# Query tokens and slot rows turned by VectorE and carried through DRAM, with a new order around the first batch's gathering

## The chip, the cores and the metric

The kernel runs on one core of one Trainium2 chip. The metric is device time in microseconds, the median of several executions; the same program runs with the same inputs each time. The profile is of one execution of its own.

## The reference

Two layers over x of shape (2, 1024, 256), all in float32. The batch is cut into four quads of 512 tokens (quads 0 and 1 are batch 0). What matters here is layer 1 and its soft mixture of experts:

```
x = x + xattn0(layernorm(x), ctx)          # layer 0, windowed attention, 8 heads
x = x + ffn0(layernorm(x))                 # layer 0, 8 groups of two linear maps
h = layernorm(x);  q = h @ Wq.T            # layer 1: 16 heads of 16
scores = sigmoid(q @ k.T * scale);  x = x + (scores @ v) @ Wo.T
xn = rms_norm(layernorm(x), gamma_x);  se = rms_norm(slot_embeds, gamma_slot)   # 1024 slots
logits   = xn @ se.T                                    # (b, s, 1024)
dispatch = softmax(logits, over tokens);  slots = dispatch.T @ xn
y        = gelu(slots @ w1) @ w2
combine  = softmax(logits, over slots);   x = x + combine @ y
```

## The kernel before

A tile holds 128 rows; a quad has QT = 4 of them, D = 256 is DC = 2 chunks of 128, and the 1024 slots are EC = 8 chunks. PSUM is used as two groups ("sides") of four banks each; a tile that needs a bank waits until an earlier user of it has been read.

Most instructions are placed on their engines by a scheduler that follows the program's order and what is ready by its own estimate. Inside `tc.manual_schedule(engines=...)` the engines named take the order of the program as it is written, and `tc.keep_in_program_order` does it for one instruction. Each engine then works its queue in order; an instruction that waits holds up those behind it. All the DMAs named here are issued by SyncE (SP), also in order.

The work in order of time (lines are those of the kernel before):

- Layer 0. `weigh` and `attend` do the attention of a quad. The two linear maps of a group are multiplied together once (`product`, L774, `pmt`), their bias follows in `bias_rows` (L805, VectorE) and `bias` (L811 to L813, `pbs` and `bs`), and `feed_forward` (L826 to L839, `po`) applies the product to `hT_f`. `layernorm` normalises a quad on VectorE (`hn`) and calls `transposed` (L126, `pt`), which turns it by eight TensorE transposes into two PSUM banks; two copies (L127) then bring it to `hT`. Who copies, ScalarE or VectorE, is left to the scheduler.
- Layer 1's attention. `layernorm(xq[q], "a1_q", 1)` makes `hT_a` for the queries of each quad, `queries` (L1150, `pq`) projects them, then for each half c of the heads: scores (L1217, `psg`, four matmuls on 32 rows each), tanh on ScalarE (`sg`, L1226), `poT` (L1251), `oT` (L1258), and `output` (L1164, `pf`) adds to x.
- Slots. `turn_slot_rows(h)` scales half of the slot embeddings (L1094) and calls `turned` (L135 and L144): VectorE transposes 32x32 squares of a tile in place, four instructions for 512 rows, and 16 DMAs of 32 KB bring the squares to the rows where they belong, as `seT`. In the attention's loop this happens once before it and once in quad 0. `turn_tokens` does the same for the tokens of each quad (`tr_m`, `xhT`).
- Logits (L224, `pl`): 128 matmul records of 512 columns with `seT` as the moving operand. VectorE reduces each bank twice (L232, L243) into row maxima and into `rmax`, the largest per slot.
- Maxima of batch 0. `largest(0)` turns `rmax` on TensorE (L296, `pm`), reduces it (L297) and multiplies it into eight diagonal 128x128 squares (L301, `dg`); `spread(0)` sums these over the rows by two matmuls with ones (L315, `pb`), which gives each row all 1024 maxima (`mb`). Then `less` (L349) adds them to the negated logits, tile by tile on GpSimd, and `dispatch` (L352) takes the exponential on ScalarE.
- Maxima of batch 1 go another way: `largest_by_moves` and `spread_by_moves` use VectorE, a DRAM row (`mrow`) and a DMA that reads the row into all partitions. For this batch `less` is on VectorE for tiles 3 and 6.
- Gathering. `gather(b, c)` (L360, `psl`) sums over the eight token tiles of a batch for slot chunk c; VectorE divides (`rz`, `sl`), `turn_slots` turns the result on TensorE (L379, `pst`) and writes `slT` with the scale (L387). During the gathering of batch 0, `turn` (L276, L285) turns the combine weights of chunks on VectorE, with 16 DMAs for each call.
- `hidden` (L435, `pmh`), `processed` and `combined` (L505, `pp` and `pc`) are fast matrix products with seven products for eight, whose sums of operands are made by `sum_slots` (L422 to L426) and others on VectorE.

Of the kernel before, what the change touches and what calls it, by code (L numbers as in the profile page):

```python
# [9 lines left out]
FP = mybir.dt.float32  # L10
AF = mybir.ActivationFunctionType
ALU = mybir.AluOpType
# [33 lines left out]
SQ = 32  # L46
R4 = P // SQ


@with_exitstack  # L50
def tile_kernel(
# [54 lines left out]

    seT = const.tile([P, 2, DC, 512], FP, tag="seT", name="seT")

# [11 lines left out]

    def transposed(src, dst, name, side=0):

        for c in range(DC):
            pt = bank(f"pt_{name}_{c}", side)
            for t in range(QT):
                nc.tensor.transpose(pt[:, ts(t, P)], src[:, t, ts(c, P)], ident)  # L126
            nc.any.tensor_copy(dst[:, c, :], pt)  # L127

    def turned(src, dst, tr, late=False):

        for t in range(QT):
            turn = nc.vector.transpose(  # L135
                tr[:, :, :, t, :].rearrange("p r c n -> p c r n"),
                src[:, t, 0:D].rearrange("p (c r n) -> p c r n", c=DC, r=R4),
            )
            if late:
                tc.keep_in_program_order(turn)  # L140
        to = dst.rearrange("p c (t i n) -> p (c t) i n", t=QT, i=R4)
        for i in range(R4):
            for r in range(R4):
                nc.sync.dma_start(  # L144
                    out=to[ts(r, SQ), :, i, :],
                    in_=tr[ts(i, SQ), r].rearrange("p c t n -> p (c t) n"),
                )


# [62 lines left out]
    def logits(b, s):  # L212
# [8 lines left out]
        for n in range(NSLOT // 512):  # L221
            pl = bank(f"pl_{b}_{s}_{n}", 0)
            for dc in range(DC):
                nc.tensor.matmul(  # L224
                    pl,
                    lhsT=xhTs[q][:, dc, ts(t, P)],
                    rhs=seT[:, n, dc, :],
                    start=(dc == 0),
                    stop=(dc == DC - 1),
                )  # L230
# [59 lines left out]
    def largest(b):  # L290

        mT = stat.tile([P, EC], FP, tag="mT", name=f"mT_{b}")
        for h in range(EC // 4):
# [5 lines left out]
            )  # L299
        dg = pools["mw"].tile([P, EC, P], FP, tag="dg", name=f"dg_{b}")  # L300
        nc.vector.tensor_tensor(  # L301
            dg,
            ident.unsqueeze(1).to_broadcast([P, EC, P]),
            mT.unsqueeze(2).to_broadcast([P, EC, P]),
            ALU.mult,
# [3 lines left out]
    def spread(b):  # L309

        dgf = mTs[b].rearrange("p c n -> p (c n)")
        mb = pools["md"].tile([P, NSLOT], FP, tag="mb", name=f"mb_{b}")
        for n in range(NSLOT // 512):
            pb = bank(f"pb_{b}_{n}", 1)
            nc.tensor.matmul(pb, lhsT=ones, rhs=dgf[:, ts(n, 512)], start=True, stop=True)  # L315
            copy(n, mb[:, ts(n, 512)], pb)
        mbs[b] = mb
# [15 lines left out]
    def spread_by_moves(b):  # L333

        w, m4 = moved[b]
        m2, m3 = w[0:SQ, 1, 5 * SQ : 6 * SQ], w[0:SQ, 1, 6 * SQ : 7 * SQ]
        tc.keep_in_program_order(
            nc.vector.tensor_reduce(m2, m4.rearrange("n i c -> n c i"), AX.X, ALU.max)
        )
        nc.vector.transpose(m3, m2)  # L340
# [6 lines left out]
    def less(b, s):  # L347
        engine = nc.vector if b == 1 and s in (3, 6) else nc.gpsimd
        engine.tensor_tensor(lgs[b][s], lgs[b][s], mbs[b], ALU.add)  # L349
# [5 lines left out]

    def gather(b, c):

        pz = bank(f"psl_{b}_{c}", 0)
        for s in range(ST):
            nc.tensor.matmul(  # L360
                pz[:, 0:XW],
                lhsT=lgs[b][s][:, ts(c, P)],
                rhs=xhs[b * QB + s // QT][:, s % QT, :],
                start=(s == 0),
                stop=(s == ST - 1),
            )
        rz = stat.tile([P, 1], FP, tag="rz", name=f"rz_{b}_{c}")
        nc.vector.reciprocal(rz, pz[:, D : D + 1])  # L368
# [60 lines left out]
    def hidden(b):  # L429
# [18 lines left out]

        p1s = [alone(0, 0)]
        turn_slots(b, EC - 1)  # L450
        p1s.append(alone(0, 1))
        p2 = alone(1, 0)
        sum_slots(b)
        hs = {}
# [263 lines left out]
    with (  # L718
# [14 lines left out]

        def layernorm(xt, name, side=0):
            mv, rstd = moments(xt, name)
            hn = lnp.tile([P, QT, D], FP, tag="hn", name=f"hn_{name}")
            for t in range(QT):
                nc.vector.tensor_scalar(  # L738
                    hn[:, t, :], xt[:, t, :], mv[:, t, 0:1], rstd[:, t : t + 1],
                    ALU.subtract, ALU.mult,  # L740
                )
            hT = lnp.tile([P, DC, QN], FP, tag="hT", name=f"hT_{name}")
            transposed(hn, hT, name, side)
            return hT
# [74 lines left out]
        def norm_ff(q, side=0):  # L819
            hTfs[q] = layernorm(xq[q], f"f0_{q}", side)  # L820

# [246 lines left out]
        with (  # L1068
# [21 lines left out]
            def turn_slot_rows(h):  # L1090
# [7 lines left out]
                tr = lnp.tile([P, R4, DC, QT, SQ], FP, tag="tr", name=f"tr_se_{h}")  # L1098
                turned(se[:, ts(h, QT), :], seT[:, h], tr, late=True)

# [42 lines left out]
            hTs, qTs, oTs = {}, {}, {}  # L1143

            def queries(q):
                qTs[q] = a1.tile([P, C1, QN], FP, tag="qT", name=f"qT_{q}")
                for c in range(C1):
                    pq = bank(f"pq_{q}_{c}", 1)
                    for dc in range(DC):
                        nc.tensor.matmul(  # L1150
                            pq,
                            lhsT=wq1s[:, dc, ts(c, P)],
                            rhs=hTs[q][:, dc, :],
                            start=(dc == 0),
# [20 lines left out]

            slot_norms()
            hTs[0] = layernorm(xq[0], "a1_0", 1)
            product(7)
            norm_ff(NQ - 1)
            turn_slot_rows(0)  # L1180
            bias_rows(7)

# [19 lines left out]
            queries(0)  # L1202
            bias(7)
            work = ExitStack()
            for q in range(NQ):
                b = q * QN // S
                oTs[q] = a1.tile([P, C1, QN], FP, tag="oT", name=f"oT_{q}")
                for c in range(C1):
                    if c == 1 and q == 0:
                        turn_slot_rows(1)  # L1210
                    if c == 0 and q > 1:
# [17 lines left out]
                    if c == 0:  # L1229
                        if q == 0:  # L1230
# [6 lines left out]
                            )  # L1237
                        if q + 1 < NQ:
                            hTs[q + 1] = layernorm(xq[q + 1], f"a1_{q + 1}", 1)
                        if q > 0:  # L1240
# [25 lines left out]

    ctx.enter_context(tc.manual_schedule(engines={mybir.EngineType.Activation}))
    open_keep(1)
    open_pool("slp", side="right")
    for u in range(1, B * ST + 2):  # L1270
        b, s = divmod(u, ST)
# [18 lines left out]

    largest_by_moves(1)
    work.close()
# [7 lines left out]
    for b in range(B):  # L1300
        slTs[b] = pools["slp"].tile([P, DC, NSLOT], FP, tag="slT", name=f"slT_{b}")
        for c in range(EC):
            gather(b, c)
            if c > 0:
                turn_slots(b, c - 1)
            if b == 0 and c in (1, 3, 5):
                turn(c // 4, c // 2 % 2, c == 5)
            if b == 1 and c % 2 == 0:
                turn(QB + c // 4, c // 2 % 2, True)
            if b == 0 and c == 0:  # L1310
                spread_by_moves(1)
                sum_weights()
            if b == 0:
                less(1, c)
                if c > 0:
                    dispatch(1, c - 1)
        if b == 0:
            dispatch(1, ST - 1)
        hidden(b)
        with tc.manual_schedule(engines={mybir.EngineType.DVE, mybir.EngineType.PE}):  # L1320
            processed(b)
            combined(b)
# [70 lines left out]
```

## Time and profile before

The median is 440.9 us (three runs, 440.69 to 441.31).

| quantity | value |
|---|---|
| profiled execution | 441.36 us |
| its span on the core | 439.6 us |
| granted TensorE clock | 1.00 |
| TensorE busy | 428.7 us (98%) |
| VectorE busy | 332.0 us (76%) |
| ScalarE busy | 113.7 us (26%) |
| GpSimd busy | 81.9 us (19%) |
| DMA packets | 101025, of them 94850 under 512 B |

In the profile PE is TensorE's matmuls, PEld its weight loads, DVE VectorE, ACT ScalarE, POOL GpSimd, and SPq the DMAs that SyncE issues. A matmul in float32 shows as two records. A matmul's record lasts longer than its share of the engine, because matmuls are pipelined; the chain of waits gives the distance from one group to the next, and that is the share. A row of the chain has the start, the length, the engine and the line. A row of a timeline has the start, the length, the instruction, and in brackets how long the engine was idle before it and what ended that. A row of the waits has the total, the number of times and the longest. A row of DMA issues has the size of one and the median time from issue to landing.

### The profile page before, as it was taken

How to read it: one execution, taken by the hardware profiler on the slowest of the kernel's cores; microseconds unless marked ns; L12 is line 12 of the kernel's file. 1: busy time of each engine (PE TensorE's matmuls, PEld its weight loads, DVE VectorE, ACT ScalarE, POOL GpSimd, SP SyncE). 2: the span in 40 equal slices, each digit the busy share in tenths (PEclk: the TensorE clock that was granted, in tenths of full speed). 3: DMA queues.
4: the chain of work that ended last, by engine and by line, in shares of the span. 5: the costliest groups of instructions: out<-in, count | busy, mean ns of one | idle time of the engine just before them, and what ended most of it. 6: DMA issues, size and time to landing. Idle time of an engine off the chain costs nothing.

```text
span 439.6 us, 6389 instructions
## 1 busy us (share of the span) xinstructions
PE 428.7 (98%) x2356; PEld 318.5 (72%) x2356; DVE 332.0 (76%) x737; ACT 113.7 (26%) x212; POOL 81.9 (19%) x82
## 2 busy tenths in 40 slices
PE   6999999999999999999999989999999999999997
PEld 5778888888755545444458854699999884499997
DVE  0477989899475766998887679995995478796856
ACT  1212143203254451333561165510000003530000
POOL 3011332224122022200695760000000000000000
PEclk9999999999999999999999999999999999999999
DMA  8996495500303032221025843333003666600002
GB/s 268 415 421 281 171 373 245 192 1 1 48 2 48 13 46 39 39 31 28 0 73 167 127 67 47 52 52 47 0 1 100 98 92 96 95 1 0 2 1 95
DMA packets 101025, 42.61 MB, mean 97 GB/s; under 512 B 94850, under 2 KB 97026, under 8 KB 99586
## 3 DMA queue, kind: packets, MB, share of 16 engines
q1 hardware_dynamic: 100994, 42.22, 36.2%
q8 instruction: 18, 0.29, 0.3%
q14 instruction: 13, 0.10, 0.1%
HBM read 28.55 MB, written 2.10 MB: 70 GB/s over the span
## 4 chain that ended last, share of the span: by engine, by line
PE 81%; DVE 14%; POOL 1%; ACT 1%; DMA 1%; issue 1%; ACTq 0%; POOLq 0%
PE psl L360 13%; PE pl L224 12%; PE pp L505 11%; PE pc L505 11%; PE pmh L435 11%; PE pmt L774 5%; DVE b2z L805 5%; PE pq L1150 3%; PE pf L1164 3%; PE psg L1217 2%; PE poT L1251 2%; PE po L832 2%; DVE hn_f L738 1%; DVE bn_f L114 1%; DVE bn_a L114 1%; PE pt_a L126 1%
## 5 line engine op out<-in xcount | busy, mean ns | idle before, releaser
L774 PE MATMUL pmt<-wg 128*128 128x256 f32 x256 | 60.3, 394 | 3.8 <-DMA wg<-in_wff_dram 3.8
L360 PE MATMUL psl<-xh,lg 128*128 128x258 f32 x256 | 58.2, 381 | 0.0
L774 PEld LDWEIGHTS pmt<-wg 128*128 128x128 f32 x256 | 50.0, 198 | 11.2 <-DMA wg<-in_wff_dram 4.3
L224 PE MATMUL pl<-seT,xhT 128*128 128x512 f32 x128 | 55.9, 593 | 0.0
L360 PEld LDWEIGHTS psl<-xh,lg 128*128 128x128 f32 x256 | 47.4, 190 | 7.2 <-issue 0.5
L224 PEld LDWEIGHTS pl<-seT,xhT 128*128 128x128 f32 x128 | 24.2, 190 | 29.1 <-issue 24.9
L349 POOL TENSOR_TENSOR lg<-lg,mb 128x1024 f32<-128x1024 f32 x14 | 34.5, 2501 | 30.4 <-DVE mb L173 26.7
L505 PEld LDWEIGHTS pp<-ms,mh 128*128 128x128 f32 x256 | 29.4, 192 | 1.0 <-issue 1.0
L505 PE MATMUL pp<-ms,mh 128*128 128x128 f32 x256 | 29.7, 276 | 0.0
L247 ACT ACTIVATE ec<-lg,nm 128x1024 f32<-128x1024 f32 x16 | 18.4, 1148 | 40.4 <-DVE nm L232 40.4
L805 DVE SCALAR_TENSOR_TENSOR b2z<-wg,fr,b2z 128x256 f32<-128x256 f32 x48 | 24.5, 515 | 0.5
L445 ACT ACTIVATE mh<-mh 128x512 f32<-128x512 f32 x32 | 19.2, 627 | 20.4 <-DVE mh L478 17.7
L435 PE MATMUL pmh<-slT,ms 128*128 128x512 f32 x48 | 24.2, 592 | 0.0
L505 PE MATMUL pp<-m_sums,mh 128*128 128x128 f32 x192 | 22.1, 275 | 0.0
L505 PE MATMUL pc<-pr,ec 128*128 128x128 f32 x192 | 22.1, 275 | 0.0
L505 PEld LDWEIGHTS pc<-pr,ec 128*128 128x128 f32 x192 | 21.8, 192 | 0.0
L505 PEld LDWEIGHTS pp<-m_sums,mh 128*128 128x128 f32 x192 | 21.8, 192 | 0.0
L352 ACT ACTIVATE lg<-lg 128x1024 f32<-128x1024 f32 x16 | 16.3, 1047 | 20.0 <-POOL lg L349 20.0
L1226 ACT ACTIVATE sg<-psg 128x512 f32<-128x512 f32 x32 | 16.5, 604 | 17.0 <-PE psg L1217 17.0
L276 DVE STREAM_TRANSPOSE tr<-ec 128x512 f32<-128x512 f32 x32 | 20.1, 679 | 0.0
L516 DVE TENSOR_TENSOR mh<-mh,mh 128x1024 f32<-128x1024 f32 x16 | 18.5, 1218 | 1.5 <-PE pp L505 1.5
L368 DVE RECIPROCAL rz<-psl 128x1 f32<-128x1 f32 x16 | 2.5, 156 | 21.5 <-PE psl L360 21.5
(192 smaller groups left out, 702.2 us busy)
## 6 DMA issues: line engine op xcount, KB each, us to landing
wg<-in_wff_dram SPq DMA_DIRECT2D x6, 2048.0 KB, 13.9
ec<-tr SPq DMA_DIRECT2D x128, 64.0 KB, 2.3
xT<-in_xT_dram SPq DMA_DIRECT2D x4, 512.0 KB, 11.4
x<-in_x_dram SPq DMA_DIRECT2D x4, 512.0 KB, 13.2
wg<-in_wff_dram SPq DMA_DIRECT2D x2, 1024.0 KB, 9.9
xhT<-tr_m SPq DMA_DIRECT2D x64, 32.0 KB, 2.0
ms<-in_m_dram SPq DMA_DIRECT2D x1, 2048.0 KB, 8.0
out_dram<-x SPq DMA_DIRECT2D x16, 128.0 KB, 1.8
```

The source lines that it names most:

```text
L224: nc.tensor.matmul(pl, lhsT=xhTs[q][:, dc, ts(t, P)], rhs=seT[:, n, dc, :], start=(dc == 0), stop=(dc == DC - 1),)
L247: nc.scalar.activation(ecs[q][:, :, t, :], lg.rearrange("p (h n) -> p h n", h=2), AF.Exp, bias=nm[:, 1:2], scale=-1.0, accum_out=zcs[b][:, ...
L276: ins = nc.vector.transpose(tr[:, :, :, t, :].rearrange("p r c n -> p c r n"), half[:, t, :].rearrange("p (c r n) -> p c r n", c=EC // 2, ...
L349: engine.tensor_tensor(lgs[b][s], lgs[b][s], mbs[b], ALU.add)
L360: nc.tensor.matmul(pz[:, 0:XW], lhsT=lgs[b][s][:, ts(c, P)], rhs=xhs[b * QB + s // QT][:, s % QT, :], start=(s == 0), stop=(s == ST - 1),)
L435: nc.tensor.matmul(to, lhsT=lefts[i][:, ts(j, P)], rhs=slTs[b][:, i, 0:512] if i < 2 else rights[b][i], start=True, stop=True,)
L445: nc.scalar.activation(h, h, AF.Gelu)
L505: nc.tensor.matmul(to, lhsT=left(k, m), rhs=right[:, k, :], start=(k == 0), stop=(k == QT - 1),)
L516: nc.vector.tensor_tensor(dst, x, y, op)
L774: nc.tensor.matmul(pm[:, ts(hc, D)], lhsT=w1g[:, oc, ts(hc, P)], rhs=w2g[:, oc, :], start=(oc == 0 and hc == 0), stop=(oc == OC - 1 and hc ...
L805: nc.vector.scalar_tensor_tensor(acc, weights[g][1][:, oc, :], b1s[:, g, oc : oc + 1], acc, ALU.mult, ALU.add)
L1226: nc.scalar.activation(sg[:, j, :], psgs[j], AF.Tanh, scale=0.5 * DH1**-0.5)
```

## The change

- The queries of layer 1 no longer pass through `transposed`. `norm_queries(q)` normalises the quad, and `turned_by_square` turns its 32x32 squares on VectorE, writes them to a DRAM tile in one DMA of 512 KB, and reads them back to their rows in four of 128 KB each. `turn_slot_rows` uses the same path, in place of 16 DMAs. The result is laid out by blocks of 32 columns, and `in_order` gives the matmuls a view of it in the order of the tokens or slots, 16 runs of 32 columns.
- Quads 0, 1 and 2 are turned before the attention's loop and quad 3 in its first pass; `turn_slot_rows(0)` comes after `bias(7)`, `turn_slot_rows(1)` one quad later than before.
- `norm_ff` of quads 2 and 3 (q >= QB) names ScalarE for its copies.
- `largest(0)` makes diagonals of 32 columns (with `ident4`, which is made once), and `spread(0)` uses four matmuls, one for each 32 rows, with four copies.
- The first three gathers of batch 0 run over token tiles 0 to 3 and then over 4 to 7. VectorE, TensorE and SP follow the written order through batch 0's gathering, `largest_by_moves(1)` stands at its head, `turn` is called at c = 1, 2 and 6 instead of 1, 3 and 5, and `less` of batch 1 is on VectorE for tiles 3, 4 and 5. The start of `hidden` is in written order too.

```diff
-    seT = const.tile([P, 2, DC, 512], FP, tag="seT", name="seT")
+    seT = const.tile([P, 2, R4, DC, QT, SQ], FP, tag="seT", name="seT")
...
+    def turned_by_square(src, dst, tr, name, late=False):
+        squares(src, tr, late)
+        by_row = dram.tile([P, R4, DC * QN // R4], FP, name=f"d_{name}")
+        nc.sync.dma_start(out=by_row, in_=tr.rearrange("p r c t n -> p r (c t n)"))
+        for r in range(R4):
+            nc.sync.dma_start(
+                out=dst[ts(r, SQ)].rearrange("p i c t n -> p i (c t n)"),
+                in_=by_row[:, r, :].rearrange("(i p) n -> p i n", i=R4),
+            )
+
+    def in_order(x, dc):
+        return x[:, :, dc].rearrange("p i t n -> p t i n")
...
-                    rhs=seT[:, n, dc, :],
+                    rhs=in_order(seT[:, n], dc),
...
-        dg = pools["mw"].tile([P, EC, P], FP, tag="dg", name=f"dg_{b}")
+        dg = diagonals[:, 0, 0 : EC * SQ].rearrange("p (c n) -> p c n", c=EC)
         nc.vector.tensor_tensor(
             dg,
-            ident.unsqueeze(1).to_broadcast([P, EC, P]),
-            mT.unsqueeze(2).to_broadcast([P, EC, P]),
+            ident4.unsqueeze(1).to_broadcast([P, EC, SQ]),
+            mT.unsqueeze(2).to_broadcast([P, EC, SQ]),
...
-        for n in range(NSLOT // 512):
-            pb = bank(f"pb_{b}_{n}", 1)
-            nc.tensor.matmul(pb, lhsT=ones, rhs=dgf[:, ts(n, 512)], start=True, stop=True)
-            copy(n, mb[:, ts(n, 512)], pb)
+        for i in range(R4):
+            r = ts(i, SQ)
+            nc.tensor.matmul(pbs[i][:, 0 : EC * SQ], lhsT=ones[r, :],
+                rhs=mTs[b][r].rearrange("p c n -> p (c n)"), start=True, stop=True)
+        for i in range(R4):
+            copy(i % 2, to[:, i], pbs[i][:, 0 : EC * SQ].rearrange("p (c n) -> p c n", c=EC))
...
-        engine = nc.vector if b == 1 and s in (3, 6) else nc.gpsimd
+        engine = nc.vector if b == 1 and s in (3, 4, 5) else nc.gpsimd
...
+        if b == 0 and c == 0:
+            for tiles in (range(4), range(4, ST)):
+                for i in range(3):
+                    gather_from(b, i, tiles)
+        elif b > 0 or c > 2:
+            gather_from(b, c, range(ST))
...
-            hTfs[q] = layernorm(xq[q], f"f0_{q}", side)
+            out = nc.any.tensor_copy if q < QB else nc.scalar.copy
+            hTfs[q] = layernorm(xq[q], f"f0_{q}", side, out)
...
-                turned(se[:, ts(h, QT), :], seT[:, h], tr, late=True)
+                turned_by_square(se[:, ts(h, QT), :], seT[:, h], tr, f"se_{h}", late=True)
...
+            def norm_queries(q, late=False):
+                hn = normed(xq[q], f"a1_{q}")
+                hTs[q] = a1.tile([P, R4, DC, QT, SQ], FP, tag="hTa", name=f"hTa_{q}", bufs=3)
+                tr = lnp.tile([P, R4, DC, QT, SQ], FP, tag="tr", name=f"tr_a_{q}")
+                turned_by_square(hn, hTs[q], tr, f"a_{q}", late)
...
-                            rhs=hTs[q][:, dc, :],
+                            rhs=in_order(hTs[q], dc),
...
-            hTs[0] = layernorm(xq[0], "a1_0", 1)
+            norm_queries(0)
             product(7)
             norm_ff(NQ - 1)
-            turn_slot_rows(0)
+            norm_queries(1)
+            norm_queries(2)
             bias_rows(7)
...
             bias(7)
+            turn_slot_rows(0)
...
                     if c == 1 and q == 0:
+                        norm_queries(3, True)
+                    if c == 1 and q == 1:
                         turn_slot_rows(1)
...
-                        if q + 1 < NQ:
-                            hTs[q + 1] = layernorm(xq[q + 1], f"a1_{q + 1}", 1)
...
+    ident4 = diagonals[:, 1, 0:SQ]
+    nc.vector.tensor_reduce(ident4, ident.rearrange("p (i n) -> p n i", i=R4), AX.X, ALU.add)
...
-    largest_by_moves(1)
...
-        for c in range(EC):
-            gather(b, c)
+        with tc.manual_schedule(engines=(IN_ORDER | {mybir.EngineType.SP}, ACT_ORDER)[b]):
+            if b == 0:
+                largest_by_moves(1)
+            for c in range(EC):
+                gather(b, c)
...
-            if b == 0 and c in (1, 3, 5):
-                turn(c // 4, c // 2 % 2, c == 5)
+                if b == 0 and c in (1, 2, 6):
+                    turn(c // 4, c // 2 % 2 if c < 4 else 0)
```

`IN_ORDER` is VectorE and TensorE, `ACT_ORDER` ScalarE alone.

## The prediction

> **What bounds the kernel now.** I read the page's first table, then the chain of waits in order of time, then what TensorE waited for. A result counts as different from 440.9 us if it is more than 0.2% (0.9 us) away, which is about what a measurement of this kernel can tell from no change.
>
> ```profile
> PE 428.7 (98%) x2356; PEld 318.5 (72%) x2356; DVE 332.0 (76%) x737; ACT 113.7 (26%) x212; POOL 81.9 (19%) x82
> ```
> ```profile
> 106.95 0.87 PE pt_a L126 x8
> ...
> 132.66 1.07 PE psg L1217 x8
> 133.72 1.02 PE pt_a L126 x8
> 134.75 3.46 PE pf L1164 x16
> ...
> 157.14 1.07 PE psg L1217 x8
> 158.21 1.92 PE pf L1164 x8
> ...
> 209.90 1.72 PE pb L315 x4
> ...
> 258.57 2.04 DVE sl_sums L422
> 260.75 21.70 PE pmh L435 x50
> ```
> ```profile
> PE pmh L435 <- DVE sl_sums L422: 1.4, 1, 1.4
> ...
> PE po L832 <- DVE hT_f L127: 0.4, 1, 0.4
> ```
>
> The first line says that TensorE is never long idle. The chain says more: from 100.6 us on it is TensorE nearly without a break, so matmul time that disappears after that point shortens the run, and work added to VectorE or to DMAs costs only where TensorE comes to wait for it. The last two lines are the two TensorE waits that the change touches.
>
> **Part A, the query transposes.** The change removes 4 x 8 = 32 TensorE transposes (`pt_a`); as built, no such instruction is left. Where nothing disturbs them, 8 take 0.87 us, 0.109 us each. Two of the four groups show 1.02 us, both just after `psg`; but at 158.21, where `pf` itself follows `psg`, 8 of its records take 1.92 us against 1.73 us elsewhere (3.46 for 16). So the extra 0.15 belongs to the step after `psg` and passes to the next matmul. I take 32 x 0.109 = 3.5 us; the end is 3.8.
>
> What takes their place lies on VectorE and SP. Per quad VectorE gets 4 stream transposes (the row for `tr_se` is 1.41 us for four) and loses a 0.67 us copy where it had one. Quads 0, 1 and 2 are turned before about 114 us, which puts 4.2 us more into VectorE's queue there; the copies that leave it or go to ScalarE (`hT_a`, and `hT_f` of quads 2 and 3) are three, 2.0 us. The cover is this, from VectorE's timeline:
>
> ```profile
> 115.28 0.69 DVE L127 COPY hT_f<-pt_f 128x512 f32<-128x512 f32 x1 [2.94 <-PE pt_f L126]
> ...
> 120.41 0.42 DVE L813 COPY bs<-pbs 128x256 f32<-128x256 f32 x1 [2.52 <-PE pbs L811]
> ...
> 123.40 0.69 DVE L839 TENSOR_TENSOR x<-x,po 128x512 f32<-128x512 f32 x1 [2.57 <-PE po L832]
> ```
>
> There are 8.0 us of idle time for 2.2 us net. Behind the turnings in VectorE's order stand `x<-x,po` of quad 2 and the `bs` copies. They release PSUM banks that TensorE next wants at about 105 us (`pv`, whose bank `bs` of group 4 frees) and 118 us (`psg`). By my count `bs` comes at 102.2 instead of 99.6 and the quad's additions end by 108, so TensorE does not wait; without that cover it would pay the 2.2 us.
>
> Then the moves. For a turned tile (seT or a quad), before: 16 issues. After: one write of 512 KB to DRAM and four reads of 128 KB, and SP waits for the write to land before the first read. Rows:
>
> ```profile
> 149.78 52.73 SPq L144 DMA_DIRECT2D xhT<-tr_m  x64
> ```
> ```profile
> seT<-tr_se SPq DMA_DIRECT2D x32, 32.0 KB, 2.0
> ...
> mb<-mrow SPq DMA_DIRECT2D x1, 512.0 KB, 5.1
> ...
> mrow<-max SPq DMA_DIRECT2D x1, 4.0 KB, 1.9
> ```
>
> The old way costs 16 x 0.61 us of issue (median of the `seT` issues) plus 2.0 us, 11.8 us. For the write the nearest rows are `out` (128 KB, 1.8 us) and `ms` (2048 KB, 8.0 us); on the line between them 512 KB take 3.0 us. `mb`, a crowded read of that size, took 5.1, and I keep 1.9 to 5.1 as ends. With four issues of at most 0.61 and a 2.0 us landing the new way takes about 7.5 us. Quads 0 to 3 are wanted by `pq` at about 115, 126, 138 and 149 us and, counted along VectorE's new order, are turned by 91, 107, 114 and 130: hidden. The tight place is behind the second seT write on SP, which now stands directly ahead of `xhT` of quad 0. VectorE finishes that half near 140.2 us; the write lands near 143.3, the reads are out by 145.7. `xhT` can start at 146.8 (149.78 less the 2.9 us gained by then) and lands 11.8 later, at 158.6; `pl` wants it at 164.23 - 3.8 = 160.4. So a landing of up to about 5.9 us costs nothing, and each us above that costs one.
>
> Here two rules of the Trainium skill speak against the change. "VectorE: DVE Perf Modes", section "Rules for kernel authors", sends 128x128 transposes to TensorE if a PSUM destination will do. It weighs one engine's time for one transpose; in this trace TensorE is the engine with none to spare. By the rule A would be worth nothing and the time would be 438.3. "DMA: Bandwidth & Descriptors", in the part on where the fixed 2 us go, warns that completion can be surprisingly long when the target is HBM; `mrow`, such a write, landed in 1.9 us. By the rule the 158.6 above slips, by the row it doesn't.
>
> A second unknown is that `pl` and `pq` now read their moving operand as 16 runs of 32 columns instead of one of 512. No row shows this. The nearest, `pk` of layer 1 (L1107), reads two runs of 64: 8 records in 0.89 us, against 0.87 for 8 unbroken `pt_a`. Ends: nothing, or 0.02/8 = 2.5 ns for each extra run, which over 15 x 160 records (128 `pl`, 32 `pq`) is 6.0 us. Unbroken 128-column groups spread from 0.109 to 0.124 us a record, so the 0.02 is within scatter and I take nothing. It can't be a gain: the columns are as many.
>
> **Part B, ScalarE copies `hT_f`.** For quad 2 TensorE waited 0.39 us for VectorE's copy, which stood behind other work until 99.9. ScalarE is done with the first copy at 99.46 and adds the second by 100.05, against 100.6. I take 0.3 (ends 0 and 0.4).
>
> **Part C, the maxima of batch 0.** `pb` was 2 matmuls (4 records) of 512 columns, 1.72 us; now it is 4 matmuls (8 records) of 256 columns on 32 rows each. The nearest row is `psg`: also 32 rows, also 8 records, 512 columns, 1.07 us. Ends: half of that, 0.54, and eight full records of 0.2145 plus 0.2 for the change of shape, 1.92. I take 0.55 plus that 0.2 = 0.75, since `psg` has the same form; gain 0.95 (ends 1.2 and -0.2). The added `ident4` reduction (about 0.3 us, as `parity`) sits in VectorE's full stretch from 172 to 200 us: 0 to 0.3, I take 0, since TensorE has four banks in hand and VectorE has caught up by 202.
>
> **Part D, the end of batch 0's gathering.** The wait of 1.37 us (260.75 less the end of `pmh` at 259.38) came from a subtraction (L422) of 2.11 us that takes 0.68 in batch 1, while GpSimd still ran this:
>
> ```profile
> 244.13 15.91 POOL L349 TENSOR_TENSOR lg<-lg,mb 128x1024 f32<-128x1024 f32 x6 [3.62 <-DMA mb<-mrow]
> ```
>
> Now the maxima of batch 1 come first on VectorE and SP, ahead of the `turn` moves: `mrow` goes out about 1.9 us earlier relative to the gathering, GpSimd has five tiles instead of six, and the subtraction stands right after the first `slT`. GpSimd should end 2.4 us before the subtraction begins, even 0.5 us before if `mb` lands as late as now. VectorE takes a third `less` (2.2 us) and the second half of the turnings before `hidden`; by my walk through its new order each `sl` is ready before the `pst` that wants it. D is 1.37 (ends 0 and 1.37). The split of the first three gathers into tiles 0-3 and 4-7 costs nothing and gains nothing: it is the same 48 records, and TensorE showed only 0.2 us of idle time in that stretch.
>
> **Sum.** 3.5 + 0.3 + 0.95 + 1.37 = 6.1 us. The profiled execution took 441.36 us (span 439.6 and 1.8 around it), so 435.3 for a like one; it lies 0.46 above the median of the runs shown, so I predict 434.8.
>
> **Rivals.**
> - Waits come back (VectorE late before 120 us, an `sl` or the `mb` late in the gathering): C or D is lost and up to 1.5 us more. For it: VectorE's full queue from 84 to 112 us, and in-order waits for DMAs in the gathering. Against it: the 8.0 us of idle time and GpSimd's 2.4 us of margin. 436.2 to 439.5, about 437.3. Chance 0.16.
> - Slower, the broken moving operand: it decides from 6.1/2400 = 2.5 ns for each extra run, 38 ns on the 429 ns of a `pl` record. For it: the 0.89 against 0.87. Against it: the scatter. At 4 ns it gives 440.9 - 6.1 + 9.6 = 444.4. Chance 0.08.
> - DRAM writes land late: at 9 us instead of 3 the first `pl` waits 3.1 us and gives 437.9. For it: 512 KB loads at 9 to 13 us in the crowded start. Against it: the page's slices show the DMA engines at most 0.3 busy from 110 to 165 us. Chance 0.04.
> - That the transposes stay on TensorE is excluded by the built order.
>
> **How the numbers follow.** The forecast has 0.72 and its own range of 433.8 to 436.2: the best ends (3.8 + 0.4 + 1.2 + 1.37 = 6.8) give 434.1, less 0.3 for scatter between runs, and the upper edge is D lost. With the first and third rival up to 438.2 the range leaves out about 2 in 10. Worst ends without the broken operand (3.5 + 0 - 0.2 + 0 - 0.3 = 3.0) give 437.9, inside it. Slower: the broken operand at 0.08 and 0.01 for the tails of the others. Same 0.03. Faster 0.88.
>
> **What would show it.** Right: no `pt_a`; `pl` still at 429 ns a record; `pb` near 0.75 us in the chain; no wait of `pmh` for `sl_sums`; the long run of `pmh` of batch 0 beginning at about 254.6 instead of 260.75. Wrong: `pl` or `pq` records above 0.44 us; TensorE waiting for `xhT`, `hTa`, `oT` or `sl`; new waits between 100 and 125 us.

## The result

The changed kernel takes 435.29 us (median of four runs, 435.02 to 435.91), beside 440.79 us for the kernel before (median of four, 440.17 to 441.31). The ratio is 0.988, with a 95% interval of 0.986 to 0.989. The profiled execution took 435.35 us with a span of 433.5 us, against 441.36 and 439.6.

The views of after, in the order of the prediction. First TensorE's, VectorE's and GpSimd's shares from the page, then the chain of waits (start, length, engine, line; line numbers are those of the changed kernel: `po` L879, `psg` L1275, `pf` L1218, `pb` L337, `pmh` L476):

```profile
PE 423.7 (98%) x2328; PEld 314.6 (73%) x2328; DVE 335.0 (77%) x751; ACT 111.8 (26%) x210; POOL 81.3 (19%) x81
```
```profile
99.31 3.58 PE po L879 x16
...
129.90 1.07 PE psg L1275 x8
130.97 3.65 PE pf L1218 x16
...
156.98 1.07 PE psg L1275 x8
158.05 1.94 PE pf L1218 x8
...
204.91 0.65 PE pb L337 x8
...
252.58 23.35 PE pmh L476 x54
```

There is no `pt_a` any more: `pf` follows `psg` directly, and it takes over the longer first step (3.65 us for 16 records, where it was 3.46). `po` is one unbroken run of 16. `pb` takes 0.65 us. The long run of `pmh` has 54 records, as it no longer breaks off after four of them for `sl_sums`; its fifth begins near 252.58 + 4 x 0.43 = 254.3 us. VectorE gained 3.0 us of work and the span fell by 6.1.

Of the waits of TensorE that the prediction showed, both are gone. One small one is new:

```profile
PE pl L245 <- DVE rmax L264: 0.2, 1, 0.2
```

The tight place on SP (start, length, instruction; the write of the second half of the slot rows, its four reads, and the first moves of the tokens), and the landings (size of one, median us from issue to landing):

```profile
139.86 0.34 SPq L159 DMA_DIRECT2D d_se<-tr_se  x1
142.89 1.73 SPq L161 DMA_DIRECT2D seT<-d_se  x4
146.18 19.20 SPq L150 DMA_DIRECT2D xhT<-tr_m  x28
```
```profile
d_a<-tr_a SPq DMA_DIRECT2D x4, 512.0 KB, 2.6
...
d_se<-tr_se SPq DMA_DIRECT2D x2, 512.0 KB, 3.8
seT<-d_se SPq DMA_DIRECT2D x8, 128.0 KB, 3.3
```

Writing to DRAM landed in 2.6 us (queries) and 3.8 us (slot rows), the reads in 2.8 and 3.3. Of the two writes of slot rows the one shown above landed sooner: it went out at 139.86 us, and the first read that waits for it at 142.89, 3.0 us later. The reads were out at 144.6. SP then waited 1.5 us for VectorE's turning of the tokens and issued their first move at 146.2 us, 0.6 earlier than forecast.

Where the 6.1 us between the two chains lie, by the starts of the same pieces:

| stretch | gained, us | predicted |
|---|---|---|
| up to `pbs` at 98 us (loads of the start) | 0.40 | 0 |
| `po` of quad 2 without its wait (B) | 0.61 | 0.3 |
| four groups of `pt_a` (A) | 3.40 | 3.5 |
| 170 to 200 us (VectorE behind `ident4`) | -0.29 | 0 |
| from `pm` to the first `psl` (C) | 0.88 | 0.95 |
| from the first `pmh` of batch 0 to `pp` (D) | 1.42 | 1.37 |
| first batch's gathering | 0.08 | 0 |
| end of `pc` to the end of the span | -0.41 | 0 |

Read like this, the sum is right, and A, C and D nearly term by term. That it also comes out at 6.1 us is luck: B gave 0.31 more than its term and `ident4` took 0.29, and the 0.40 of the start and the -0.41 of the end, which no term had, cancel too. The experiments show that such a table of differences is not a table of prices.

### The profile page after: what moved, and what is told of

It is laid out like the page before. It is cut to its first block, busy times and chain, and to the rows that moved or that the text cites. A ratio compares the mean times of both kernels' runs of the same rounds, so it can differ in the third digit from the quotient of the medians.

```text
span 433.5 us, 6357 instructions
## 1 busy us (share of the span) xinstructions
PE 423.7 (98%) x2328; PEld 314.6 (73%) x2328; DVE 335.0 (77%) x751; ACT 111.8 (26%) x210; POOL 81.3 (19%) x81
## 4 chain that ended last, share of the span: by engine, by line
PE 84%; DVE 11%; POOL 1%; ACT 1%; issue 1%; DMA 1%; DVEq 0%; ACTq 0%
PE psl L390 13%; PE pp L547 12%; PE pc L547 12%; PE pmh L476 11%; PE pmt L820 10%; PE pl L245 7%; PE pq L1204 3%; PE pf L1218 3%; PE po L879 2%; DVE b2z L851 2%; PE psg L1275 2%; PE poT L1307 2%; DVE lg L253 1%; PE psc L1029 1%; DVE hn_f L780 1%
## 5 line engine op out<-in xcount | busy, mean ns | idle before, releaser
L376 POOL TENSOR_TENSOR lg<-lg,mb 128x1024 f32<-128x1024 f32 x13 | 33.2, 2597 | 26.8 <-ACT mb L192 25.3
L476 PE MATMUL pmh<-slT,ms 128*128 128x512 f32 x48 | 24.2, 592 | 0.0
L547 PE MATMUL pc<-pr_sums,ec 128*128 128x128 f32 x160 | 18.5, 275 | 0.0
```

The lines of the kernel that those rows point to most:

```text
L476: nc.tensor.matmul(to, lhsT=lefts[i][:, ts(j, P)], rhs=slTs[b][:, i, 0:512] if i < 2 else rights[b][i], start=True, stop=True,)
L547: nc.tensor.matmul(to, lhsT=left(k, m), rhs=right[:, k, :], start=(k == 0), stop=(k == QT - 1),)
```

## The experiments

All times are medians; "before" was run beside each and lay at 440.5 to 440.8 us.

**1. Part A alone.** The kernel before, with only the queries' way changed (and `dg` in another tile, whose old place the queries' tiles take):

```diff
-            hTs[0] = layernorm(xq[0], "a1_0", 1)
+            norm_queries(0)
             product(7)
             norm_ff(NQ - 1)
+            norm_queries(1)
+            norm_queries(2)
...
-                            hTs[q + 1] = layernorm(xq[q + 1], f"a1_{q + 1}", 1)
```

> The kernel before with part A alone: the query tokens are turned on VectorE and go by way of DRAM, `pq` reads them as runs of 32; slot rows, maxima, gathering and the copies of hT_f stay as before (the diagonals lie in another tile, since the memory they had is taken). Theory (the terms add up, and A is the 32 transposes at 0.109 us): 3.4 to 3.5 us less than 440.8, so 437.3 us, no pt_a in the chain, the wait of 1.4 us for sl_sums and pb at 1.72 us still there. Rival 1 (the gain comes from the new order around the gathering): within 0.9 us of 440.8. Rival 2 (A only pays together with the other parts, because VectorE's turnings then hold up TensorE before 120 us or SP's queue delays xhT): 438.5 to 440, with a new wait of TensorE between 100 and 165 us.

443.2 us, ratio 1.009 (1.005 to 1.012): slower than before. Every theory missed the sign. TensorE's longest waits in this kernel:

```profile
PE po L866 <- DVE hT_f L127: 3.9, 1, 3.9
...
PE pmh L465 <- DVE sl_sums L452: 2.1, 1, 2.1
```

And the end of the chain that leads to the first of them:

```profile
103.17 0.34 DVE bs L847
103.51 0.61 DVE hT_f L127
...
104.16 4.97 PE po L866 x14
```

The copy of `hT_f` of quad 2, which VectorE still makes here, ends at 104.1 us, 3.9 us after `po` wanted it. VectorE's timeline has it 3.5 us later than in the kernel before (99.88):

```profile
96.61 0.73 DVE L768 TENSOR_SCALAR hn_f<-x,mv_f,rstd_f 128x256 f32<-128x256 f32 x2 [0.93 <-POOL rstd_f L118]
...
103.42 0.68 DVE L127 COPY hT_f<-pt_f 128x512 f32<-128x512 f32 x1
```

The turning of quad 0 takes 1.4 us of that. The rest is `hn_f` of quad 3, which stood behind the copy (at 100.47) and now stands ahead of it, with 1.3 us of work and 0.9 us of idle time. What follows costs again: the next 14 records of `po` take 4.97 us, where 16 take 3.58 undisturbed. (Two of the five executions were 2.5 and 3.8 us above the median. One of them is the profiled one, which had a second drop of the clock, after the wait for `sl_sums`, worth 1.7 us. The other left no trace; its mean clock is the same, 0.992, where the other three have 0.995 or 0.996.)

**2. Parts A and B.** Experiment 1 with ScalarE named for the copies of `hT_f` in quads 2 and 3:

```diff
+            out = nc.any.tensor_copy if q < QB else nc.scalar.copy
-            hTfs[q] = layernorm(xq[q], f"f0_{q}", side)
+            hTfs[q] = layernorm(xq[q], f"f0_{q}", side, out)
```

> The kernel before with parts A and B: query tokens by VectorE and DRAM, and hT_f of quads 2 and 3 copied by ScalarE. Part A alone took 443.2 us, 2.4 more than before instead of 3.4 less: TensorE waited 3.9 us for the VectorE copy of hT_f, which stood behind the new turnings until 104.1, and then ran at a granted clock of 0.65 for 4 us. New theory (B is the cover that A needs, so A and B are one term): that wait is gone, A gives its 3.4 us and B its 0.6, so 436.8 us, with the wait for sl_sums (1.4 to 2.1 us) and pb at 1.72 us still there; 437.5 if one of the sums waits over 2 us again. Rival 1 (VectorE's queue is too full whoever copies, and the wait moves to bs, oT or x): 439 to 442. Rival 2 (part A pays only with the slot rows by DRAM as well, since SP's 16 moves collide): a wait of pl for xhT, 438 to 440.

437.47 us, ratio 0.993 (0.991 to 0.995). The wait for `hT_f` is gone and A pays. The median is 0.7 us above the theory's 436.8. The profiled execution, the longest of the four with 438.26 us, shows where such a rest lies: a new wait of 0.6 us (`pf` for `oT`), and waits for `sl_sums` of 1.7 + 0.5 us against 1.4 before.

**3. The changed kernel without B.**

```diff
-            out = nc.any.tensor_copy if q < QB else nc.scalar.copy
+            out = nc.any.tensor_copy
```

> The changed kernel with part B undone: who copies hT_f is left to the scheduler again, and VectorE gets one copy of quad 2 and one of quad 3; all else as changed. Theory (without B, part A's turnings stand ahead of the copy): TensorE waits 3 to 4 us for hT_f at 100 us and runs slower for some 4 us after, 1.5 to 2 us more: 440 to 441.5 us. Rival 1 (B is a small term by itself, as the prediction had it): 435.6 to 435.9, wait of at most 0.4 us. Rival 2 (in the changed order the copy finds an earlier place): 435.3.

440.38 us (ten runs), ratio 0.9996 (0.9986 to 1.0006): these copies left to the scheduler give back the whole 5 us. TensorE waits 3.9 us for `hT_f`, whose copy begins on VectorE at 102.24 us (the second row is of the chain):

```profile
PE po L879 <- DVE hT_f L129: 3.9, 1, 3.9
```
```profile
102.24 0.61 DVE hT_f L129
```

The view by windows (busy time of each engine, granted clock, DMA share, GB/s) shows what comes after:

```profile
103.00:104.00 1.00, 1.00 (x4) 0.82 (x5) 1.00 (x2) 0.00 (x0) 1.00 (x2) 0.69 0.00 0
104.00:105.00 1.00, 1.00 (x4) 0.82 (x3) 1.00 (x2) 0.00 (x0) 0.85 (x1) 0.50 0.00 0
105.00:106.00 1.00, 1.00 (x3) 0.76 (x3) 1.00 (x5) 0.00 (x0) 0.00 (x0) 0.50 0.00 0
106.00:107.00 1.00, 1.00 (x4) 0.84 (x3) 1.00 (x4) 0.00 (x0) 0.00 (x0) 0.61 0.00 0
```

The wait ended at 102.9 us. The granted clock (third number from the end) is 1.00 while TensorE idles, falls to 0.50 once it has work again, and is 1.00 from 107 us on. Its missing parts add up to 0.31 + 0.50 + 0.50 + 0.39 = 1.70 us. So this wait costs 3.9 + 1.7 = 5.6 us of TensorE. The medians differ by 5.1, and this execution had reached `po` 0.95 us earlier than the profiled one of the changed kernel (98.36 against 99.31).

**4. B for quad 2 alone.**

```diff
-            out = nc.any.tensor_copy if q < QB else nc.scalar.copy
+            out = nc.scalar.copy if q == QB else nc.any.tensor_copy
```

> The changed kernel with ScalarE named for the copies of hT_f of quad 2 alone; for quad 3 the scheduler gives one of the two copies to VectorE, ahead of the turning of the third quad. Theory (B's price is that of one copy, hT_f of quad 2, which po wants at 99 us while VectorE is behind): 435.3 us, no wait for hT_f. Rival (quad 3's copy, wanted by po at 119 us, stands behind VectorE's turnings too): a wait of po for hT_f near 119 us, 436 to 441 us.

435.17 us, ratio 0.988 (0.986 to 0.989), as the theory has it. VectorE's copy for quad 3 stands at 114.68 us, and `po` does not wait for it. The whole price of B is one copy of 0.68 us that must not stand in VectorE's queue at 100 us.

**5. The old moves, and an unbroken moving operand.** The queries and the slot rows go by 16 direct moves of 32 KB, as `turned` does, so that `pq` and `pl` read rows of 512:

```diff
-                    rhs=in_order(seT[:, n], dc),
+                    rhs=seT[:, n, dc, :],
...
-        nc.sync.dma_start(out=by_row, in_=tr.rearrange("p r c t n -> p r (c t n)"))
-        for r in range(R4):
+        for i in range(R4):
+            for r in range(R4):
+                nc.sync.dma_start(
+                    out=dst.rearrange("p c (t i n) -> p (c t) i n", t=QT, i=R4)[ts(r, SQ), :, i, :],
+                    in_=tr[ts(i, SQ), r].rearrange("p c t n -> p (c t) n"),
+                )
```

> The changed kernel with 16 direct moves of 32 KB (runs of 128 bytes) in place of the write to DRAM and four reads, for the queries and the slot rows, so that pq and pl read unbroken rows of 512. Theory (a moving operand of 16 runs costs nothing; the way through DRAM only has to be early enough): pl stays at 429 ns and pq at 3.6 us for 8; SP spends 5.4 to 9.8 us on the 16 issues of the second slot half instead of 3 to 5, so xhT starts at 146 to 150 us and the first pl waits 0 to 2 us: 435.3 to 437.3 us. Rival 1 (the broken operand costs something that the sum hides): pl and pq get shorter, 1 us less for each 0.4 ns a run, below 434.5. Rival 2 (the moves through DRAM are what makes the change possible): SP falls behind in the queries too, pq waits for hTa, over 438 us.

447.54 us, ratio 1.017 (1.015 to 1.018): rival 2. SP's queue from 99.9 to 162.8 us is one row of 83 moves for queries and slot rows, 0.65 us each (10.39/16) where nothing holds it, and the tokens' begin at 163 us instead of 146 (three of its five rows):

```profile
99.86 31.08 SPq L160 DMA_DIRECT2D hTa<-tr_a  x35
...
152.05 10.79 SPq L160 DMA_DIRECT2D seT<-tr_se  x16
162.95 12.38 SPq L150 DMA_DIRECT2D xhT<-tr_m  x19
```

TensorE waits 5.3 us for `xhT`, 2.9 for `oT` and 0.5 for `hTa`, with the clock at 0.50 after the first two. The operand is settled too. Here 72 undisturbed records of `pl` took 30.90 us in the chain, 429 ns each, as before and as in the changed kernel. The group of `pl` in the changed kernel (busy time, mean ns of one record, idle time before):

```profile
L245 PE MATMUL pl<-seT,xhT 128*128 128x512 f32 x128 | 56.1, 594 | 0.2 <-DVE rmax L264 0.2
```

Before, with one run of 512, the mean was 593 ns, and it is 593 in experiment 8 too, which has the runs of 32; for `pq` it is 605 ns before and in the changed kernel. Sixteen runs of 32 cost nothing.

**6. Direct moves with long runs.** The same 16 moves, but into the changed layout, so that each partition moves 1 KB in a row:

```diff
+                nc.sync.dma_start(
+                    out=dst[ts(r, SQ), i].rearrange("p c t n -> p (c t n)"),
+                    in_=tr[ts(i, SQ), r].rearrange("p c t n -> p (c t n)"),
+                )
```

> The changed kernel with the way through DRAM replaced by 16 direct moves of one 32x32-block row each, 32 KB, that keep the changed layout, so that each partition moves one run of 1 KB (the moves that kept the old layout had runs of 128 bytes, took SP 0.61 us each and gave 447.5 us). pq and pl read the operand as runs of 32, as in the changed kernel. Theory (SP's time goes by the number of runs, not of moves): an issue takes 0.3 to 0.4 us, a quad 5 to 6.4 us instead of 0.34 + 2.4 of waiting + 1.73, nothing waits, 435.3 us, perhaps a wait of 0 to 1 us of the first pl for xhT. Rival (SP's time goes by the number of moves): 0.6 us each again and 445 to 448 us.

451.03 us, ratio 1.023 (1.020 to 1.026). My theory fell. Sixteen such moves took SP 10.03 us, 0.63 each, nearly as long as those with runs of 128 bytes (10.39 us). SP's time goes by the number of these moves. That this is even slower than experiment 5 does not come from SP: its order is the same, and the tokens' moves begin 0.9 us earlier (162.03 against 162.95). The trace puts it in TensorE's order. In experiment 5 the last rows of TensorE ahead of `pl` end with twelve records of `pf` (first row), so that the work of the attention is done before the wait; here they stand behind `pl`, and the wait of 9.8 us holds them up too (second row):

```profile
166.57 2.91 PE L1217 MATMUL pf<-w1s,oT 128*128 128x256 f32 x12
```
```profile
173.97 6.67 PE L244 MATMUL pl<-seT,xhT 128*128 128x512 f32 x8 [9.81 <-DMA xhT<-tr_m]
```
What the way through DRAM buys is not a quicker landing but five issues instead of sixteen: for the second slot half 0.34 + 1.73 us of SP and 2.7 of waiting for the landing, instead of 10.

**7. A second hop.** Each tile is copied once more inside DRAM between the write and the reads:

```diff
-        nc.sync.dma_start(out=by_row, in_=tr.rearrange("p r c t n -> p r (c t n)"))
+        first = dram.tile([P, R4, DC * QN // R4], FP, name=f"d1_{name}")
+        nc.sync.dma_start(out=first, in_=tr.rearrange("p r c t n -> p r (c t n)"))
+        nc.sync.dma_start(out=by_row, in_=first)
```

> The changed kernel with every turned tile copied once more inside DRAM (512 KB from one DRAM tile to another) between the write and the four reads. Theory (the landing of the DRAM write has slack: the prediction put it at 2.9 us for the second slot half, and more for the queries): the copy lands in 2.5 to 5 us, the reads start that much later; 435.3 us if it takes under 3 us, up to 437.5 with a wait of pl for xhT if it takes 5. Rival 1 (the changed kernel already stands at its margin): each us of the copy is paid, 438 to 440, and pq waits for hTa. Rival 2 (the copy is hidden whatever it takes): 435.3 with xhT starting as in the changed kernel.

441.41 us (ten runs), ratio 1.001 (0.999 to 1.003): above what any of the theories allowed. The queries take the copy (4.4 us to its landing) without a wait. The tokens' moves stand 4.4 us later on SP (150.55 us), and the first `pl` waits:

```profile
163.38 2.05 PE L247 MATMUL pl<-seT,xhT 128*128 128x512 f32 x2 [3.91 <-issue]
```

The row names no releaser, but the view of the tile `xhT` does: `pl` waited 3.9 us for its moves. Of the sixteen, fifteen stand from 150.55 us on; one of them took SP 1.87 us, the others about 0.65, so that the last goes out at 161.0 and, with 2.0 us to its landing, is there at 163.0. This chain is 0.4 us ahead of the changed kernel's, so the delay against it is 4.8 us and the slack of the tokens' moves 0.9. The slack of the landing in DRAM is larger, since SP had waited 1.5 us for the tokens in the changed kernel: about 2.4 us together. The clock is at 0.50 from about 162 to 169 us. Nine of ten executions lie between 440.6 and 441.8 us with a mean granted clock of 0.991 or 0.992; the tenth kept 1.00 and took 437.48, and left no trace.

**8. The old maxima.** Diagonals of 128 columns, `pb` as two matmuls of 512 columns, no `ident4`:

```diff
-            ident4.unsqueeze(1).to_broadcast([P, EC, SQ]),
+            ident.unsqueeze(1).to_broadcast([P, EC, P]),
...
-        for i in range(R4):
+        for n in range(NSLOT // 512):
+            pb = bank(f"pb_{b}_{n}", 1)
+            nc.tensor.matmul(pb, lhsT=ones, rhs=dgf[:, ts(n, 512)], start=True, stop=True)
```

> The changed kernel with batch 0's maxima spread as before: diagonals of 128 columns and pb as two matmuls of 512, no ident4. Theory: C comes back, 0.88 us (the step from pm to the first psl), and the 0.29 us that TensorE lost behind ident4 goes; net 0.6 us more than 435.3, so 435.9 us, pb at 1.7 us in the chain, and the step from pf to pm shorter by 0.3 us. Rival 1 (the lag of VectorE after 170 us has another cause than ident4): 436.2 us with the lag still there. Rival 2 (the shorter pb is hidden, as VectorE and GpSimd set the start of the gathering): 435.3 us.

435.84 us, ratio 0.989 (0.988 to 0.990). The medians differ by 0.55 us, inside the intervals; the chain decides. From `pm` at 199.40 to the first `psl` at 222.59 are 23.19 us, where the changed kernel has 22.31, and the wait of `pl` for `rmax` is gone. Both 0.88 and -0.29 are right.

**9. The old gathering.** Order, split, `turn` and `less` of batch 0's gathering as before:

```diff
-        with tc.manual_schedule(engines=(IN_ORDER | {mybir.EngineType.SP}, ACT_ORDER)[b]):
-            if b == 0:
-                largest_by_moves(1)
...
-        engine = nc.vector if b == 1 and s in (3, 4, 5) else nc.gpsimd
+        engine = nc.vector if b == 1 and s in (3, 6) else nc.gpsimd
```

> The changed kernel with batch 0's gathering as in the kernel before: no written order for VectorE, TensorE and SP, gathers over all eight tiles at once, turn at c = 1, 3 and 5, largest_by_moves ahead of the loop, less of tiles 3 and 6 on VectorE. Theory (D is the order of the gathering): the wait of pmh for sl_sums comes back at about 1.4 us, 436.7 us, GpSimd's run of six less ends after the first sl_sums has begun. Rival 1 (D came from the queues standing earlier since A took the transposes away): no such wait, 435.3 us. Rival 2 (the written order also costs something in the gathering, which the old one saves): 435.5 to 436.2 with the wait back.

437.17 us, ratio 0.992 (0.990 to 0.994). The wait is back at 1.9 us, and so is its cause in the chain:

```profile
253.04 2.92 DVE sl_sums L463
...
256.10 1.11 PE pmh L476 x2
```

GpSimd works its six tiles from 239.49 for 15.91 us, to 255.4, and the subtraction beside it takes 2.92 us. In the changed kernel GpSimd is done at 251.5, and the same subtraction takes 0.69:

```profile
236.90 14.60 POOL L376 TENSOR_TENSOR lg<-lg,mb 128x1024 f32<-128x1024 f32 x5 [1.56 <-DMA mb<-mrow]
```

**10. The old `less` in the new order.** Everything else as changed:

```diff
-        engine = nc.vector if b == 1 and s in (3, 4, 5) else nc.gpsimd
+        engine = nc.vector if b == 1 and s in (3, 6) else nc.gpsimd
```

> The changed kernel with less of batch 1 on VectorE for tiles 3 and 6, as before, instead of 3, 4 and 5; the written order, the split gathers and the early maxima stay. Theory (GpSimd's last less decides, and it ends when its tiles are done): GpSimd has six tiles from about 236.9 to 252.8 us, 1.3 us later than with five and past the start of sl_sums at 253.1 less its own length; between 0.2 and 1 us of D comes back, 435.5 to 436.3 us. Rival 1 (the early maxima alone give all of D): 435.3. Rival 2 (the shift of less alone gives all of D): a wait of 1.4 us or more for sl_sums, 436.7 or above.

436.70 us, ratio 0.992 (0.990 to 0.994), with executions from 435.76 to 439.45. The size is rival 2's, the place is nobody's. The profiled execution, the longest and the only one with a drop of the clock (mean 0.996, the others 0.999 or 1.00), has no wait for `sl_sums` but this:

```profile
251.30 2.84 DVE lg L376
...
254.26 0.49 DVE sl L411
...
254.79 0.69 PE pst L420 x2
```

In the written order `less` of tile 6 stands ahead of the last `sl`, late and beside GpSimd, and `pst` waits 2.6 us. Tiles 4 and 5 on VectorE come earlier, where it has time. What the early maxima give without any move of `less` was not run.

**11. `ident4` made early.** The reduction moves to quad 0's attention, into the tile that `mb` takes later:

```diff
-    ident4 = diagonals[:, 1, 0:SQ]
+                            ident4 = pools["md"].tile([P, NSLOT], FP, tag="mb", name="ident4")[:, 0:SQ]
```

> The changed kernel with ident4 made early, during quad 0's attention, where VectorE has idle time, instead of after layer 1's attention. Theory (the 0.29 us that TensorE lost between 170 and 200 us is VectorE's lag behind that reduction of 0.37 us): the wait of pl for rmax (0.2 us) goes, 435.0 us. Rival 1 (the lag has another cause, the norm of quad 2's tokens at that place): 435.3 with the wait still there. Rival 2 (the reduction delays something of quad 0 instead): over 435.6.

434.70 us, ratio 0.986 (0.985 to 0.988). The wait of 0.2 us for `rmax` is gone, which is the theory's mark, and from `pf` at 156.84 us to `pm` at 198.26 are 41.42 us, where the changed kernel has 41.70 (158.05 to 199.75). The 0.6 us between the medians is more than the 0.3 expected and within scatter.

**12. One turning more.** Experiment 11, and `hT_f` of quad 3 by VectorE as well. That is 8 transposes fewer on TensorE and two copies fewer on ScalarE, 1.4 us more on VectorE, and 16 moves of 32 KB more on SP, at the 0.63 us of experiment 6. ScalarE makes the `bs` copies of groups 4 to 7, and SP takes the moves of quads 3, 1 and 2 in written order:

```diff
+            hn = normed(xq[q], f"f0_{q}")
+            hTfs[q] = lnp.tile([P, DC, QN], FP, tag="hT", name=f"hT_f0_{q}")
+            tr = lnp.tile([P, R4, DC, QT, SQ], FP, tag="tr", name=f"tr_f_{q}")
+            turned(hn, hTfs[q], tr)
...
-            nc.any.tensor_copy(bs, pb[:, 0:D])
+            (nc.any.tensor_copy if g < 4 else nc.scalar.copy)(bs, pb[:, 0:D])
```

> [...] Theory (TensorE's time is the bound and VectorE and SP have room between 98 and 115 us): the moves are issued from 100.5 to 110.6 us and land by 112.6, po wants them at 118.6; 0.87 us less than with ident4 early alone, 434.1 us. Rival (that room is already used up, as part A without B showed): TensorE waits over 2 us somewhere between 100 and 125 us and its granted clock falls after it, 438 to 441 us.

433.90 us, ratio 0.985 (0.984 to 0.986): it beats both kernels, 1.4 us below the changed one. SP issues these moves where it had been idle, ahead of those for quad 1:

```profile
99.49 11.01 SPq L150 DMA_DIRECT2D hT_f<-tr_f  x16
110.61 0.54 SPq L159 DMA_DIRECT2D d_a<-tr_a  x1
```

No wait of TensorE is over 0.2 us after 100 us. The `bs` copies went to ScalarE so that none could stand behind VectorE's turning of quad 1, as `hT_f` did behind other work in experiment 1; what they would have cost there was not run.

## Why the prediction was right, and where it was not

The time (434.8 against 435.29) and the sign came from the right mechanism: matmul time that goes after 100 us shortens the run, and three of the four terms stand in the chain with nearly their size.

- **A** gave 3.40 us for 3.5. The extra 0.15 after `psg` did pass on to `pf` (3.65 us for 3.46). But the cover that the prediction named, three idle stretches of VectorE between 113 and 123 us, was not what decided. It put `bs` at 102.2 us, which held (102.60), and the end of the quad's additions by 108, where it was 110.4 without a wait, and looked only at PSUM banks behind them. The copy of `hT_f`, wanted at 99 to 100 us, stood just behind `bs` in a queue without B (102.24 in experiment 3). "Without that cover it would pay the 2.2 us" named the wrong cover and the wrong price: without B the changed kernel pays 5.1 us (440.38 less 435.29).
- **B** is the step that failed. It was priced by the wait it removes from the kernel before (0.3 us, 0.61 measured), not by the wait it keeps away in the kernel after. Alone, A costs 2.6 us; with B the two gain 3.0. They are one term, and the sum of the prediction was right only because both were in the change. That the forecast held in this point is luck: B was in the change, but for another reason than the one it was priced by.
- **C** gave 0.88 for 0.95, for the reason told. **D** gave 1.42 for 1.37, in the main for the reason told too: with the old gathering the wait is back (experiment 9), and GpSimd ended 1.6 us ahead of the subtraction (251.5 against 253.14) for the 2.4 forecast. How much of D the early maxima give by themselves is open. `ident4`, put at 0 with an end of 0.3, cost 0.29: the four banks in hand did not cover it.
- **The moving operand** was rightly put at nothing; the slower rival is excluded, at 594 against 593 ns a record.
- **The way through DRAM** landed as estimated (2.6 to 3.8 us for 3.0, and 3.0 in the tight place), the reads later (2.8 to 3.3 for 2.0). The slack behind it was about right: 2.9 us by the prediction, some 2.4 by experiment 7, but otherwise divided. SP had 1.5 us to spare ahead of the tokens' moves, where 1.1 were forecast, and the moves 0.9 instead of 1.8: SP takes 19.20/28 = 0.69 us for one at that place instead of 0.61, and `pl` begins at 159.8 instead of 160.4. And "each us above that costs one" is wrong: above some 2 us of wait it can cost 1.7 or 3.4 more.
- **The two rules** that spoke against the change: the one on transposes (the Trainium skill, "VectorE: DVE Perf Modes", section "Rules for kernel authors") gave 438.3 us with A worth nothing. The runs side with the row of the trace, 3.40 us, as long as VectorE's queue has the room; where it had not, in experiment 1, the rule's outcome was the better one. The warning on DRAM writes (the Trainium skill, "DMA: Bandwidth & Descriptors", section "Anatomy of one DMA — SWDGE (gpsimd) path", which is about DMAs that GpSimd issues) did not bite: 512 KB landed in 2.6 to 3.8 us where the sum had 3.0, and nothing waited. The 1.4 us of `mrow` are for 4 KB.
- **The first rival**, waits that come back, was priced at up to 1.5 us. Its true price, had VectorE been late in one more place, is about 5 us, beyond the upper end of the range.

## What to carry to other kernels

A part of a change that looks small may be the cover of the large one, so price it in the kernel after: follow the new queue in order past the place, and ask for every instruction behind it when its reader wants it. On a kernel like this one, which TensorE bounds, a wait of more than about 2 us can cost 1.7 us on top of its length, so it matters more to have none of that size than to save a little on many. Where SP's queue decides, count the issues, not the bytes.

## What the runs showed of the hardware

What a long wait costs beyond its length is the granted clock. After idle times of TensorE of 1.4 and 1.9 us (the kernel before, experiment 9) it stayed at 1.00; after 2.06 us in experiment 1, 2.6 us in experiment 10, and 2.9 us and more in others it went to 0.50, mostly once TensorE was busy again; after 2.4 us in experiment 6 it did not. (The start is left aside: TensorE is idle for the first 3.8 us of the changed kernel's span, the records show 1.00 there and after it, and yet the first 32 records of `pmt` take 9.80 us where later ones take 7.07. Why is open.) Two windows of experiment 1, whose wait of 2.06 us ended at 264.55:

```profile
266.00:267.00 1.00, 1.00 (x3) 0.47 (x2) 0.33 (x1) 0.00 (x0) 0.00 (x0) 0.50 0.00 0
...
268.00:269.00 1.00, 1.00 (x2) 0.39 (x2) 0.77 (x2) 0.00 (x0) 0.00 (x0) 0.50 0.00 0
```

With 0.90 in the window before them, 0.50 between them and 0.89 after them, the missing parts are 0.10 + 3 x 0.50 + 0.11 = 1.71 us, as the 1.70 of experiment 3: half the clock for 3.4 us. In experiment 7 they add up to twice that, with part of it inside the wait. The Trainium skill, "TensorE: Matmul & The Clock Gate", Part 1, says that the clock is halved after an idle window of about 3.4 us and that the window runs freely and does not begin anew with the kernel. The length agrees with the 3.4 us here. But a whole idle window was not needed, since 2.06 us was enough once. A window that runs freely would fit that 2.06 us brought the drop where 2.4 us did not, and that one execution in ten of experiment 7 kept its clock; no run shows that this is the cause. That execution took only 2.2 us more than the changed kernel, so its wait may also have been shorter.

A move of 32 KB from SBUF to SBUF on 32 partitions took SP 0.63 us with runs of 1 KB and 0.65 to 0.69 with runs of 128 bytes, while a read of 128 KB from DRAM took 1.73/4 = 0.43 and a write of 512 KB 0.34. I had not expected the small moves to be the dear ones. The three kinds differ in where they read and write and in the partitions they span, and no run shows which of these sets the price.
